# Moving a transpose from the matrix engine to VectorE and DMA in a two-layer graph kernel

## The chip, the cores and the metric

The kernel runs on one core of one Trainium2 chip. The metric is the device time of one execution in microseconds. Three executions of the kernel before took 2980.95 to 2983.51 us, with a median of 2982.35 us.

## What is computed

64 graphs of 256 nodes with 512 features, all in float32. Layer 0 is a graph network of three steps, layer 1 an attention whose weights are a softmax over the nodes; each layer ends with a residual sum and a layer norm.

```python
def _gcn_layer(x, adj, W, b):
    support = jnp.einsum('bnf,fh->bnh', x, W)
    return jnp.einsum('bnm,bmh->bnh', adj, support) + b

# layer 0
h = relu(_gcn_layer(x, adj, W1, b1)); h = relu(_gcn_layer(h, adj, W2, b2))
x1 = layernorm(x + _gcn_layer(h, adj, W3, b3))

# layer 1
q, k = split(x1 @ Wqk); v = x1 @ Wv
agg = einsum('bij,bjd->bid', adj, k * mask[:, :, None])
w = inv_scale * mask * einsum('bid,bid->bi', q, agg)
out = layernorm(x1 + softmax(w, axis=1)[:, :, None] * v)
```

The kernel uses q k^T = x1 M x1^T with M = Wq Wk^T, computed once. A score is then a row sum of (x1 M x1^T) times the adjacency.

## The kernel before

The graphs go through in 32 pairs (G = 2), one pair a pass, in a software pipeline over two pairs: pass i does layer 0 of pair i and, interleaved with it, the end of layer 0 and all of layer 1 of pair i-1. There is one pass more than there are pairs. Nodes are cut into NH = 2 halves of 128, features into DC = 4 chunks of 128.

A product of a pair with a 512x512 weight matrix is done by `seven` (L123 and L141 to L158): a Strassen-Winograd scheme with seven block products of four 128x128x256 products each, in place of eight. The left operand's sums S1, S2, S3, S4 are made by `left` (L108 to L111) on VectorE (DVE) and GpSimd (POOL); the weights' sums are constant. In `seven` the banks are X, Y, W, Z (bx, by, bw, bz). X is added to three times; after each time ScalarE (ACT) copies it out (u L141, v L147, t L152) before PE may add more, and DVE adds such a copy to Y, W, Z and writes the four quarters of the result. The quarter written last is the one of the bw drain (L158), which follows the last block product; the one before it comes from bz (L156).

The steps of a pass on TensorE (PE), in the order of the source:

- project W1 for pair i (L123), then pp (L199): the third adjacency product of pair i-1, 512 columns wide, drained and normalized by DVE in `layer0_out` and `layernorm` (L184 to L201) into x1, held in the tile xt
- pz (L175): the first adjacency product of pair i, drained with relu by ACT into hT
- px (L212): x1 of pair i-1 transposed on PE against an identity, 16 blocks of 128x128, copied out by ACT into x1T (L213)
- project W2 of pair i, then x1 M of pair i-1 (yT), then pz of the second step, then pg (L223), the scores' product yT x1T, whose drain on DVE (L228) makes w
- project W3 of pair i, then the softmax over the nodes: pw (L236, two small transposes), nmax on DVE (L238), e on ACT (L241, an exp), smx on DVE; then x1 Wv (vs), then ps (L251, the softmax back into columns), and on DVE `layer1_out`: the weighted sum, the layer norm and the store of xt to out (L262)

So each projection is followed on PE by a product that doesn't read its result, and each adjacency product by one that doesn't read its own.

Tiles come from pools with a fixed number of buffers: s, xt, an and mr have two, aT three, xT, x1T, yT, c and hT one. PSUM has seven banks with the tag "mm", taken in turn. The order of instructions on every engine is fixed when the kernel is built: a scheduler merges the steps and inserts waits on semaphores. All loads and stores are issued by SyncE (SP), in order. A DMA is counted on one of eight DMA semaphores in turn, so the ninth waits until the first has landed.

Of the kernel before, what the change touches and what calls it, by code (L numbers as in the profile page):

```python
# [9 lines left out]
FP = mybir.dt.float32  # L10
AF = mybir.ActivationFunctionType
OP = mybir.AluOpType
AX = mybir.AxisListType

P = 128
# [3 lines left out]
@with_exitstack  # L19
def gcn_then_graph_attention(ctx: ExitStack, tc: tile.TileContext, xT, xn, adjT, adjn, mask_row, mask_col,  # L20
                             W1, b1, W2, b2, W3, b3, WqT, WkT, Wv, out):

# [12 lines left out]
    nc = tc.nc  # L37
    NP, _, DC, G, N = xT.shape
    NH = N // P
    D = DC * P  # L40
    H = D // 2
# [6 lines left out]
    work = ctx.enter_context(tc.tile_pool(name="work", bufs=1))  # L48
# [39 lines left out]
    def load_w(w, name, eng):  # L88
        t = const.tile([P, 7, 2, H], FP, name=name)
        b12 = work.tile([P, 2, H], FP, name="b12", tag="t", bufs=2)  # L90
        nc.sync.dma_start(t[:, B11], w[:, 0:2, 0:H])
        nc.sync.dma_start(b12, w[:, 0:2, H:D])
        nc.sync.dma_start(t[:, B21], w[:, 2:4, 0:H])
        nc.sync.dma_start(t[:, B22], w[:, 2:4, H:D])
        combine_w(t, b12, eng)
        return t

# [1 line left out]

    def left(src, own, eng1, eng2, name, bufs=1):  # L100

        A11, A21 = src[:, 0:2, :, 0:P], src[:, 0:2, :, P:N]
        A12, A22 = src[:, 2:4, :, 0:P], src[:, 2:4, :, P:N]
        n = 4 if own else 3
        c = work.tile([P, n, 2, G, P], FP, name=name, bufs=bufs)
        S1, S2, S4 = c[:, 0], c[:, 1], c[:, 2]
        S3 = c[:, 3] if own else A21
        eng1.tensor_tensor(S1, A21, A22, op=OP.add)  # L108
        eng2.tensor_tensor(S3, A11, A21, op=OP.subtract)  # L109
        eng1.tensor_tensor(S2, S1, A11, op=OP.subtract)  # L110
        eng2.tensor_tensor(S4, A12, S2, op=OP.subtract)  # L111
        return dict(A11=A11, A12=A12, A22=A22, S1=S1, S2=S2, S3=S3, S4=S4)
# [14 lines left out]
    def seven(lf, w, dst, nodes_out):  # L127

        def bank(name):
            return psum.tile([P, 2, H], FP, name=name, tag="mm")  # L130

        def view(x):
            return x if nodes_out else x.rearrange("p o (g n) -> p o g n", g=G)

        def temp(name):
            return work.tile([P, 2, H], FP, name=name, tag=name, bufs=2)

        X = bank("bx")
        product(X, lf["A11"], w[:, B11], True, False, nodes_out)
        u = temp("u")  # L140
        nc.scalar.copy(u, X)  # L141
        Y = bank("by")
        product(Y, lf["A12"], w[:, B21], True, True, nodes_out)
        nc.vector.tensor_tensor(dst(0, 0), view(Y), view(u), op=OP.add)
        product(X, lf["S2"], w[:, T2], False, False, nodes_out)
        v = temp("v")
        nc.scalar.copy(v, X)  # L147
        W = bank("bw")
        product(W, lf["S3"], w[:, T3], True, False, nodes_out)
        product(X, lf["S1"], w[:, T1], False, True, nodes_out)  # L150
        t = temp("t")
        nc.scalar.copy(t, X)  # L152
        nc.vector.tensor_tensor(dst(1, 1), view(W), view(t), op=OP.add)  # L153
        Z = bank("bz")
        product(Z, lf["S4"], w[:, B22], True, True, nodes_out)
        nc.vector.tensor_tensor(dst(0, 1), view(Z), view(t), op=OP.add)  # L156
        product(W, lf["A22"], w[:, N4], False, True, nodes_out)
        nc.vector.tensor_tensor(dst(1, 0), view(W), view(v), op=OP.add)  # L158

    def project(lf, w, name, bufs):  # L160

        s = work.tile([P, G, NH, D], FP, name=name, bufs=bufs)
        seven(lf, w, lambda h, o: s[:, :, h, o * H:(o + 1) * H], True)
        return s


# [26 lines left out]

    def layer0_out(s, aT, xt):
        for g in range(G):
            for h in range(NH):
                pp = psum.tile([P, D], FP, name="pp", tag="mm")
                for m in range(NH):
                    nc.tensor.matmul(pp, lhsT=aT[:, g, m, h * P:(h + 1) * P], rhs=s[:, g, m, :],  # L199
                                     start=(m == 0), stop=(m == NH - 1))  # L200
                nc.vector.tensor_tensor(xt[:, g, h, :], pp, xt[:, g, h, :], op=OP.add)  # L201
            layernorm(xt, g)

    def transpose_x1(x1):
        x1T = work.tile([P, DC, G, N], FP, name="x1T")
        for g in range(G):
            for fp in range(DC // 2):
                pt = psum.tile([P, 2, N], FP, name="px", tag="mm")
                for j in range(2):
                    f = 2 * fp + j  # L210
                    for h in range(NH):
                        nc.tensor.transpose(pt[:, j, h * P:(h + 1) * P], x1[:, g, h, f * P:(f + 1) * P], ident)  # L212
                nc.scalar.copy(x1T[:, 2 * fp:2 * fp + 2, g, :], pt)  # L213
        return x1T

    def scores(i, yT, x1T, an):

        w = small.tile([P, NH, G], FP, name="w", bufs=2)
        for g in range(G):
            pg = psum.tile([P, NH, N], FP, name="pg", tag="mm")  # L220
            for h in range(NH):
                for d in range(DC):
                    nc.tensor.matmul(pg[:, h, :], lhsT=yT[:, d, g, h * P:(h + 1) * P], rhs=x1T[:, d, g, :],  # L223
                                     start=(d == 0), stop=(d == DC - 1))
            for h in range(NH):
                prod = work.tile([P, N], FP, name="prod")
                b = i * G + g
                nc.vector.scalar_tensor_tensor(prod, pg[:, h, :], mask_s[:, h, b:b + 1], an[:, g, h, :],  # L228
                                               op0=OP.mult, op1=OP.mult, accum_out=w[:, h, g:g + 1])
        return w  # L230
# [25 lines left out]
    def layer1_out(i, x1, v, s):  # L256
        for g in range(G):
            for h in range(NH):
                nc.vector.scalar_tensor_tensor(x1[:, g, h, :], v[:, g, h, :], s[:, h, g:g + 1], x1[:, g, h, :],
                                               op0=OP.mult, op1=OP.add)  # L260
            layernorm(x1, g)
        nc.sync.dma_start(out[i], x1)  # L262
# [34 lines left out]
    def make_m():  # L297
        b12 = work.tile([P, 2, H], FP, name="b12", tag="t", bufs=2)
        for f in range(DC):
            pt = psum.tile([P, 2, H], FP, name="pt", tag="mm")  # L300
            for d in range(DC):
                nc.tensor.matmul(pt, lhsT=qT[:, d, f * P:(f + 1) * P], rhs=kT[:, d, :],  # L302
                                 start=(d == 0), stop=(d == DC - 1))
            nc.scalar.copy(wm[:, B11 if f < 2 else B21, f % 2], pt[:, 0])
            nc.scalar.copy(b12[:, f % 2] if f < 2 else wm[:, B22, f % 2], pt[:, 1])
        combine_w(wm, b12, nc.gpsimd)

    V, PL = nc.vector, nc.gpsimd  # L310
    prev = None
    for i in range(NP + 1):
        new = i < NP
        if new:
            s = project(lx, w1, "s", 2)
        if prev is not None:
            xt, an = rest
            layer0_out(prev, aTs[i - 1], xt)
        if new:
            if i + 1 < NP:  # L320
                x0 = load_xT(i + 1)
                aTs[i + 1] = load_aT(i + 1)
            hT = aggregate_relu(s, aTs[i], bl1)
        if prev is not None:
            x1T = transpose_x1(xt)
        if new:
            s = project(left(hT, False, V, PL, "ch"), w2, "s", 2)
            if i + 1 < NP:
                lx = left(x0, False, PL, PL, "cx")
        if prev is not None:  # L330
            l1 = left(x1T, True, V, PL, "c1")
            yT = work.tile([P, DC, G, N], FP, name="yT")
            seven(l1, wm, lambda h, o: yT[:, 2 * o:2 * o + 2, :, h * P:(h + 1) * P], False)
        if new:
            hT = aggregate_relu(s, aTs[i], bl2)
        if prev is not None:
            w = scores(i - 1, yT, x1T, an)
        if new:
            s = project(left(hT, False, V, PL, "ch"), w3, "s", 2)
        if prev is not None:  # L340
            sm = softmax_rows(w)
            v = project(l1, wv, "vs", 1)
            layer1_out(i - 1, xt, v, softmax_cols(sm))
        if new:
            rest = load_rest(i)
        if i == 0:
            make_m()
        prev = s


# [40 lines left out]
```

## Time and profile before

The profiled execution took 2982.62 us, its span on the core 2980.8 us, at a mean granted TensorE clock of 0.996.

| group of the profile | count | busy us | mean ns |
|---|---|---|---|
| PE px, transposes (L212) | 512 | 74.9 | 283 |
| ACT x1T, their copies (L213) | 128 | 68.4 | 589 |
| PE pp, 512 columns (L199) | 512 | 225.1 | 592 |
| PE pz, 256 columns (L175) | 2048 | 453.6 | 379 |
| DVE L191, last step of the layer norm | 256 | 276.8 | 1123 |
| POOL L72, bias into xt | 32 | 145.4 | 4544 |
| DMA out, 1024 KB each | 32 | | 3900 to landing |

How to read it: each row is a group of instructions of one line; busy is their sum, the mean is one instruction's length as recorded. Matmuls are pipelined, so their recorded lengths overlap, and what a step takes is read from the starts of the steps in the timeline. A float32 product shows up as two instructions, a transpose as one. Over the span the 16 DMA engines are busy with 13.6% for the queue that SP issues on, and moved 149.24 MB there in 32864 packets.

### The profile page before, as it was taken

The page shows a single profiled execution, that of the slowest core. Times are in us where ns is not written, and L with a number is a line of the kernel's source. Part 1 is how long each engine was busy: PE and PEld are TensorE (multiplying, and loading weights), DVE is VectorE, ACT ScalarE, POOL GpSimd, SP SyncE. Part 2 cuts the span into 40 slices and gives each one's busy share as a digit, 9 for nine tenths or more (in the row PEclk, how much of TensorE's full clock was granted, in tenths as well). Part 3 has the DMA queues.
Part 4 walks back from the last instruction along what each step waited for, and adds up shares of the span by engine and source line. Part 5 has one row for each costly group of instructions (what it writes and reads, how often), then busy time and mean ns, then how long its engine had stood idle before and what let it go on. Part 6 is the DMA issues. An engine that isn't in the chain of part 4 may idle for free.

```text
span 2980.8 us, 32161 instructions
## 1 busy us (share of the span) xinstructions
PE 2926.8 (98%) x13216; PEld 2442.2 (82%) x13216; DVE 1363.5 (46%) x2386; ACT 661.5 (22%) x1130; POOL 698.1 (23%) x426
## 2 busy tenths in 40 slices
PE   8999999999999999999999999999999999999997
PEld 6788888888888888888888888888888888888885
DVE  3355334554345543455543455434555345554344
ACT  1222122222222222222212222222222122221221
POOL 4222022221222221222202222112222122221210
PEclk9999999999999999999999999999999999999998
DMA  5011101111011110111110111101111011111000
GB/s 195 22 61 61 46 25 57 53 61 60 11 60 50 60 61 26 45 57 54 60 54 18 60 50 60 61 11 60 50 61 60 32 39 57 53 60 50 8 29 28
DMA packets 33010, 151.29 MB, mean 51 GB/s; under 512 B 3680, under 2 KB 7904, under 8 KB 20320
## 3 DMA queue, kind: packets, MB, share of 16 engines
q1 hardware_dynamic: 32864, 149.24, 13.6%
q8 instruction: 104, 1.70, 0.2%
q14 instruction: 42, 0.34, 0.0%
HBM read 115.68 MB, written 33.55 MB: 50 GB/s over the span
## 4 chain that ended last, share of the span: by engine, by line
PE 90%; DVE 8%; DMA 1%; issue 1%; ACT 1%; POOL 0%; SPq 0%; DVEq 0%; POOLq 0%
PE bx L123 28%; PE bw L123 18%; PE pz L175 10%; PE bz L123 9%; PE by L123 9%; PE pg L223 7%; PE pp L199 6%; DVE xt L191 5%; DVE st L184 1%; PE px L212 1%; DVE xt L201 1%; DMA w<-in_W 1%; PE pt L302 0%; DMA xt<-in_xn 0%; DVE mv L185 0%
## 5 line engine op out<-in xcount | busy, mean ns | idle before, releaser
L175 PE MATMUL pz<-aT,s 128*128 128x256 f32 x2048 | 453.6, 379 | 0.0
L175 PEld LDWEIGHTS pz<-aT,s 128*128 128x128 f32 x2048 | 389.7, 190 | 66.7 <-issue 14.8
L109 POOL TENSOR_TENSOR hT<-hT 128x512 f32<-128x512 f32 x64 | 113.0, 1766 | 880.9 <-DVE ch L108 880.9
L108 POOL TENSOR_TENSOR cx<-xT 128x512 f32<-128x512 f32 x32 | 40.6, 1269 | 1024.9 <-DMA xT<-in_xT 990.0
L191 DVE TENSOR_SCALAR xt<-xt,mv,rs 128x512 f32<-128x512 f32 x256 | 276.8, 1123 | 1.2
L177 ACT ACTIVATE hT<-pz,bl 128x512 f32<-128x512 f32 x256 | 175.2, 685 | 400.8 <-PE pz L175 400.7
L123 PE MATMUL bw<-w,hT 128*128 128x256 f32 x1024 | 242.0, 379 | 1.6 <-POOL hT L109 1.6
L123 PE MATMUL bx<-w,ch 128*128 128x256 f32 x1024 | 242.0, 379 | 0.0
L153 DVE TENSOR_TENSOR s<-bw,t 128x512 f32<-128x512 f32 x96 | 66.4, 692 | 361.9 <-ACT t L152 361.9
L141 ACT COPY u<-bx 128x512 f32<-128x512 f32 x160 | 93.6, 585 | 612.7 <-PE bx L123 612.7
L223 PE MATMUL pg<-x1T,yT 128*128 128x256 f32 x1024 | 226.2, 379 | 0.0
L199 PE MATMUL pp<-s,aT 128*128 128x512 f32 x512 | 225.1, 592 | 0.0
L123 PEld LDWEIGHTS bw<-w,hT 128*128 128x128 f32 x1024 | 189.5, 190 | 33.4 <-POOL hT L109 2.0
L123 PEld LDWEIGHTS bx<-w,ch 128*128 128x128 f32 x1024 | 194.5, 190 | 26.6 <-issue 0.2
L223 PEld LDWEIGHTS pg<-x1T,yT 128*128 128x128 f32 x1024 | 194.6, 190 | 26.5
L152 ACT COPY t<-bx 128x512 f32<-128x512 f32 x160 | 93.6, 585 | 454.7 <-PE bx L123 447.4
L199 PEld LDWEIGHTS pp<-s,aT 128*128 128x128 f32 x512 | 97.2, 190 | 108.8 <-issue 107.1
L147 ACT COPY v<-bx 128x512 f32<-128x512 f32 x160 | 93.6, 585 | 406.5 <-PE bx L123 406.5
L184 DVE BATCH_NORM_STATS2 st<-xt 128x6 f32<-128x512 f32 x256 | 170.6, 688 | 2.1
L72 POOL TENSOR_TENSOR xt<-xt,bl 128x2048 f32<-128x2048 f32 x32 | 145.4, 4544 | 53.5 <-DMA xt<-in_xn 53.5
L108 DVE TENSOR_TENSOR ch<-hT 128x512 f32<-128x512 f32 x64 | 43.9, 686 | 234.5 <-ACT hT L177 234.5
L75 POOL TENSOR_TENSOR an<-an,mr 128x512 f32<-128x512 f32 x64 | 79.8, 1267 | 209.5 <-DMA an<-in_adjn 202.4
(108 smaller groups left out, 4543.2 us busy)
## 6 DMA issues: line engine op xcount, KB each, us to landing
xT<-in_xT SPq DMA_DIRECT2D x32, 1024.0 KB, 4.8
xt<-in_xn SPq DMA_DIRECT2D x32, 1024.0 KB, 6.9
out<-xt SPq DMA_DIRECT2D x32, 1024.0 KB, 3.9
aT<-in_adjT SPq DMA_DIRECT2D x32, 512.0 KB, 3.4
an<-in_adjn SPq DMA_DIRECT2D x32, 512.0 KB, 3.5
mr<-in_mask_row SPq DMA_DIRECT2D x32, 256.0 KB, 3.1
w<-in_W SPq DMA_DIRECT2D x9, 256.0 KB, 6.4
qT<-in_WqT SPq DMA_DIRECT2D x1, 1024.0 KB, 6.9
```

What stands on the lines that cost most here:

```text
L72: nc.gpsimd.tensor_tensor(xt.rearrange("p g h d -> p (g h) d"), xt.rearrange("p g h d -> p (g h) d"), bl3.unsqueeze(1).to_broadcast([P, G ...
L109: eng2.tensor_tensor(S3, A11, A21, op=OP.subtract)
L123: nc.tensor.matmul(bank[:, o], lhsT=lhsT, rhs=rhs, start=first and n == 0, stop=last and n == 3, skip_group_check=True)
L141: nc.scalar.copy(u, X)
L147: nc.scalar.copy(v, X)
L152: nc.scalar.copy(t, X)
L175: nc.tensor.matmul(pz[:, g, :], lhsT=s[:, g, m, f * P:(f + 1) * P], rhs=aT[:, g, m, :], start=(m == 0), stop=(m == NH - 1))
L177: nc.scalar.activation(hT[:, f], pz, AF.Relu, bias=bias[:, f:f + 1])
L184: nc.vector.bn_stats(st[:, h, :], x[:, g, h, :])
L191: nc.vector.tensor_scalar(x[:, g, h, :], x[:, g, h, :], mv[:, h, 0:1], rs[:, h:h + 1], op0=OP.subtract, op1=OP.mult)
L199: nc.tensor.matmul(pp, lhsT=aT[:, g, m, h * P:(h + 1) * P], rhs=s[:, g, m, :], start=(m == 0), stop=(m == NH - 1))
L223: nc.tensor.matmul(pg[:, h, :], lhsT=yT[:, d, g, h * P:(h + 1) * P], rhs=x1T[:, d, g, :], start=(d == 0), stop=(d == DC - 1))
```

## The change

x1 is no longer transposed on PE. In the new `transpose_x1` DVE transposes the 32x32 blocks of each 128x512 tile, each block where it stands (four instructions a pass, into the tile xs), and 16 DMAs from SP, each for one pair of partition groups, move the blocks to where a full transpose puts them (x1T). Each of these DMAs covers 32 partitions with 16 runs of 32 floats, from SBUF to SBUF. xs shares its buffer with yT. The layout of x1T changes from chunk, graph, node to graph, half, chunk, node, and `left` and `scores` index it so.

Softmax, x1 Wv and the rest of layer 1 become `attention_out` and are done one pass later, after the first pz of the next pass; the loop has one pass more. The source order of a pass is then W1, pp, pz, the late `attention_out`, W2, `transpose_x1`, pz, x1 M, W3, scores.

The column halves of every weight are loaded swapped and written swapped, so that `seven` completes columns 0 to 255 with its third drain and columns 256 to 511 with its fourth. pp runs in two halves of 256 columns, the first half of both node halves first.

```diff
-        nc.sync.dma_start(t[:, B11], w[:, 0:2, 0:H])
-        nc.sync.dma_start(b12, w[:, 0:2, H:D])
-        nc.sync.dma_start(t[:, B21], w[:, 2:4, 0:H])
-        nc.sync.dma_start(t[:, B22], w[:, 2:4, H:D])
+        nc.sync.dma_start(t[:, B11], w[:, 0:2, H:D])
+        nc.sync.dma_start(b12, w[:, 0:2, 0:H])
+        nc.sync.dma_start(t[:, B21], w[:, 2:4, H:D])
+        nc.sync.dma_start(t[:, B22], w[:, 2:4, 0:H])
...
-        seven(lf, w, lambda h, o: s[:, :, h, o * H:(o + 1) * H], True)
+        seven(lf, w, lambda h, o: s[:, :, h, (1 - o) * H:(2 - o) * H], True)
...
     def layer0_out(s, aT, xt):
         for g in range(G):
+            pps = [psum.tile([P, D], FP, name="pp", tag="mm") for h in range(NH)]
+            for o in range(2):
+                for h in range(NH):
+                    for m in range(NH):
+                        nc.tensor.matmul(pps[h][:, o * H:(o + 1) * H], lhsT=aT[:, g, m, h * P:(h + 1) * P],
+                                         rhs=s[:, g, m, o * H:(o + 1) * H], start=(m == 0), stop=(m == NH - 1))
             for h in range(NH):
-                pp = psum.tile([P, D], FP, name="pp", tag="mm")
-                for m in range(NH):
-                    nc.tensor.matmul(pp, lhsT=aT[:, g, m, h * P:(h + 1) * P], rhs=s[:, g, m, :],
-                                     start=(m == 0), stop=(m == NH - 1))
-                nc.vector.tensor_tensor(xt[:, g, h, :], pp, xt[:, g, h, :], op=OP.add)
+                nc.vector.tensor_tensor(xt[:, g, h, :], pps[h], xt[:, g, h, :], op=OP.add)
             layernorm(xt, g)
 
     def transpose_x1(x1):
-        x1T = work.tile([P, DC, G, N], FP, name="x1T")
+        Q = 32
+        xs = work.tile([P, G, NH, DC, P // Q, Q], FP, name="xs", tag="yT")
         for g in range(G):
-            for fp in range(DC // 2):
-                pt = psum.tile([P, 2, N], FP, name="px", tag="mm")
-                for j in range(2):
-                    f = 2 * fp + j
-                    for h in range(NH):
-                        nc.tensor.transpose(pt[:, j, h * P:(h + 1) * P], x1[:, g, h, f * P:(f + 1) * P], ident)
-                nc.scalar.copy(x1T[:, 2 * fp:2 * fp + 2, g, :], pt)
+            for h in range(NH):
+                nc.vector.transpose(xs[:, g, h].rearrange("p c b n -> p (c b n)"), x1[:, g, h, :])
+        x1T = work.tile([P, G, NH, DC, P], FP, name="x1T")
+        for nb in range(P // Q):
+            for fb in range(P // Q):
+                nc.sync.dma_start(
+                    x1T[fb * Q:(fb + 1) * Q, :, :, :, nb * Q:(nb + 1) * Q].rearrange("p g h c n -> p (g h c) n"),
+                    xs[nb * Q:(nb + 1) * Q, :, :, :, fb, :].rearrange("p g h c n -> p (g h c) n"))
         return x1T
...
-    prev = None
-    for i in range(NP + 1):
+    def attention_out(i, l1, xt, w):
+        sm = softmax_rows(w)
+        v = project(l1, wv, "vs", 1)
+        layer1_out(i, xt, v, softmax_cols(sm))
+
+    prev, late = None, None
+    for i in range(NP + 2):
...
-        if prev is not None:
-            x1T = transpose_x1(xt)
+        if late is not None:
+            attention_out(*late)
+            late = None
         if new:
             s = project(left(hT, False, V, PL, "ch"), w2, "s", 2)
             if i + 1 < NP:
                 lx = left(x0, False, PL, PL, "cx")
         if prev is not None:
+            x1T = transpose_x1(xt)
+        if new:
+            hT = aggregate_relu(s, aTs[i], bl2)
+        if prev is not None:
             l1 = left(x1T, True, V, PL, "c1")
             yT = work.tile([P, DC, G, N], FP, name="yT")
-            seven(l1, wm, lambda h, o: yT[:, 2 * o:2 * o + 2, :, h * P:(h + 1) * P], False)
-        if new:
-            hT = aggregate_relu(s, aTs[i], bl2)
+            seven(l1, wm, lambda h, o: yT[:, 2 - 2 * o:4 - 2 * o, :, h * P:(h + 1) * P], False)
+        if new:
+            s = project(left(hT, False, V, PL, "ch"), w3, "s", 2)
         if prev is not None:
             w = scores(i - 1, yT, x1T, an)
-        if new:
-            s = project(left(hT, False, V, PL, "ch"), w3, "s", 2)
-        if prev is not None:
-            sm = softmax_rows(w)
-            v = project(l1, wv, "vs", 1)
-            layer1_out(i - 1, xt, v, softmax_cols(sm))
+            late = (i - 1, l1, xt, w)
```

In the order as built, a steady pass has on SP six of the 16 block moves, then the store to out, then the other ten, then the loads of xt, an and mr; on DVE the four block transposes stand before nmax, and nmax before the copies for W2's left sums; on POOL the bias addition into xt stands after the sums c of x1T.

## The prediction

> **What bounds the kernel now.** I read the busy shares first, then PE's waits, then one pass in the timeline.
>
> ```profile
> span 2980.8 us, 32161 instructions
> ...
> PE 2926.8 (98%) x13216; PEld 2442.2 (82%) x13216; DVE 1363.5 (46%) x2386; ACT 661.5 (22%) x1130; POOL 698.1 (23%) x426
> ```
>
> PE is busy 98% of the span and no other engine half of it. The view of waits, cut to PE, holds only this:
>
> ```profile
> PE px L212 <- DVE xt L191: 19.3, 30, 1.5
> PE bx L123 <- DMA w<-in_W: 7.3, 1, 7.3
> PE px L212 <- issue: 5.8, 1, 5.8
> PE bw L123 <- DVE s L153: 3.7, 1, 3.7
> PE bw L123 <- POOL hT L109: 1.6, 1, 1.6
> ```
>
> So a change pays only if it takes work from PE or makes PE wait. The only repeated wait, 30 times, stands before the transposes px. The timeline of one pass, PE alone, from project W1 (start 995.80) on:
>
> ```profile
> 1008.00 7.03 PE L199 MATMUL pp<-s,aT 128*128 128x512 f32 x16
> 1014.86 7.07 PE L175 MATMUL pz<-aT,s 128*128 128x256 f32 x32
> 1021.77 1.04 PE L212 MATMUL px<-ident,xt 128*128 128x128 f32 x8
> 1023.25 1.44 PE L212 MATMUL px<-ident,xt 128*128 128x128 f32 x8 [0.45 <-DVE xt L191]
> 1024.53 1.89 PE L123 MATMUL bx<-w,hT 128*128 128x256 f32 x8
> ```
>
> The transposes hold PE from 1021.77 to 1024.53, 2.76 us with their wait. The next pass begins at 1087.22: 91.42 us a pass, 32 such passes. Other lengths from starts in the same view: a projection of 28 products 12.1 us, pz or pg 6.9, pp 6.86.
>
> **What the Trainium skill says.** "VectorE: DVE Perf Modes", The three transpose paths: VectorE transposes 32x32 blocks only, 311 ns for a 128x128 bf16 tile; no transpose on VectorE is in this trace. "DMA: Bandwidth & Descriptors", Specifications: below 512 B a transfer is read, modified and written; its section Why small descriptors are slow says that SBUF to SBUF does not suffer, 128-byte packets still reaching 78% of the link. The two pull apart, and nothing here is 128 B. The same page, Queues, rings and completion order: each DMA engine consumes its descriptors in ring order. "TensorE: Matmul & The Clock Gate", Part 1: after an idle window of some 3.4 us the array runs at half clock for about as long. The trace agrees: PE idles from 21 to 24.7 us, and the stretches 26 to 29 us show a granted clock of 0.50.
>
> **The change part by part.** Times below are inside one steady pass, 0 where W1 starts.
>
> *Transposes off PE.* 16 px a pass go: -2.76. pp becomes 32 products of 256 columns instead of 16 of 512; pz has that form and takes 6.91 against 6.86: +0.05. Net -2.71, times the 31 passes that have a following W2: -84. ACT loses four copies of 0.59, which nobody waited for.
>
> *New order on PE.* W1 0, pp 12.2, pz 19.1, pw 26.0, x1Wv of the pass before 26.3 to 38.4, ps, W2 38.6 to 50.7, pz 50.7 to 57.6, x1M 57.6, W3, pg. Formerly x1M lay between W2 and the pz that reads its result; now pz follows W2 directly. The swapped halves deal with that: columns 0 to 255 are complete with the bz drain, which in the trace is done 0.9 us after bz, and the last product bw takes 1.73; pz's first two groups then take 3.46 while bw drains. Cost 0. The same few drains sit behind layer 1's chain on DVE, as they did behind W1 before (bz drained at 1006.47, bw ended 1008.16), so this cover holds.
>
> *Softmax before x1Wv.* The exp e stands on ACT ahead of u, the copy of x1Wv's first bank, and PE may add into that bank again only after u. Two products cover it: u must be done by 26.3+3.46 = 29.8. e waits for nmax, and DVE has nmax behind all four transposes. DVE: first add 14.9 (its bank is now full after 6 of 8 product groups), group 0 normalized by 21.3, as long as before since POOL's cx still collides with it (2.62 us for the L191 pair at 1014.68); group 1 adds and statistics to 24.1; two transposes; the L191 pair now about 1.0 since POOL's xt addition L72 (4.52 us, which stretched it to 4.25) has moved behind c; two transposes. A transpose of 128x512: the skill's 311 ns less 133 for 128 columns at one a cycle leaves 178, plus 533 gives 0.71 (estimate); bn_stats of the same size takes 0.69. So nmax starts about 28.3, e 28.7 (ACT: hT, then a table load of 1.28, also till 28.7), its 0.65, u 0.58: 30.0. I charge 0.4 a pass. Bounds: 0, and 2.6 if a transpose takes two cycles a column (1.3).
>
> *Block moves.* 16 DMAs a pass, each 32 partitions x 16 rows of 128 B, all from SP's queue. x1T has one buffer, last read by x1Wv, so they start at its end, E = 38.4. In the built order six go, then out, then ten. The out waits for layer 1:
>
> ```profile
> 1085.19 1.89 PE L123 MATMUL bw<-wv,x1T 128*128 128x256 f32 x8
> 1087.72 0.15 DVE L253 COPY s<-ps 128x4 f32<-128x4 f32 x1
> 1094.85 0.99 DVE L191 TENSOR_SCALAR xt<-xt,mv,rs 128x512 f32<-128x512 f32 x2
> 1095.87 0.34 SPq L262 DMA_DIRECT2D out<-xt  x1
> ```
>
> That is (bw done at 1087.1) 8.8 us after x1Wv, and the ten blocks stand behind it on SP. Cutting the DMA view to 1095 to 1099.5 shows out's data until 3.2 us after its issue; the engines take the blocks after that: E+12.0. The ten are 320 rows per engine. Each engine's price d of a 128 B row: in the saturated stretch 5 to 20 us,
>
> ```profile
> DMA packets 3690, 5.49 MB, mean 366 GB/s; under 512 B 517, under 2 KB 3305, under 8 KB 3433
> ...
> q1 hardware_dynamic: 3690, 5.49, 102.9%
> ```
>
> 1.029x16x15 = 247 engine-us; at the 437 GB/s that the adjn load peaks at, 27.3 per engine, the bytes take 201; the other 46 over 3690 packets are 12.5 ns each, and 128 B adds 4.7: 17 ns. Read-modify-write might double it: 34. Below: 5, bytes alone. Above: the lone loads of 2 KB (15.5% of 16 engines over 7 us, 144 packets: 121 ns) and 4 KB (26.5% over 6 us, 144: 177 ns) give by a straight line 65 at nothing, so about 68. I take 22, above the saturated figure because of the skill's remark. The last block lands at E+12.0+0.32d+0.6 = E+19.6. x1M wants x1T at 57.6 = E+19.2. Stall 0.4. Issue is no limit: ten of about 0.45 (128 rows 0.34, 256 rows 0.38 at start) from E+9.2. DVE (c, L108) and POOL (c, L109) wait at the heads of their queues for the same landing; behind them are only yT drains and the next xt addition. S2 needs 1.25+1.65 after landing, PE gives it 3.46. SP sits on the first block from about 19 to E; the next loads (xt, an) come behind the blocks and are due a pass later.
>
> *The end.* After the last layer 0 nothing is left to run under the moves. Before: pp end (2924.65) to 2980.8 is 56.2, plus the x1Wv that stood ahead of pp, 12.3: 68.5. After: x1Wv 12.1 and about 2.8 for a copy late behind two table loads, 19.6 for the blocks, x1M 12.1 and 1.5 for the halved clock, pg 6.9, x1Wv 12.5, DVE and out 13.1: 80.6. So +12.
>
> **Sum.** The profiled execution took 2982.6, 0.3 above the median of the runs. 2982.6-84+12 = 2910.6; 30 passes have both stalls, 30x(0.4+0.4) = 24: 2935. Break-even is at 2.4 us of stall a pass.
>
> **Rivals.**
>
> *A. Blocks late behind out.* For: the margin is nothing, one SP wait holds ten of the sixteen, and the row size is not in the trace. The stall is 0.32d-6.6 a pass; it decides from d = 27, where it is 2.0 and together with the 0.4 reaches break-even. At d = 34 it is 4.3, and about 1.7 more once the array has cooled: 2910.6+30x6.4 = 3103. At 68 it is 15.2+1.7: some 3430. Against: the saturated stretch says 17. Chance 0.30.
>
> *B. Softmax late.* Transposes at two cycles: 2910.6+30x(2.6+0.4) = 3001. For: e ahead of u on ACT. Against: bn_stats at a column a cycle. Chance 0.06.
>
> *C. Both about 1 us too long*, 2910.6+30x2.4 = 2982: no change. Chance 0.05.
>
> *D. Nothing waits*: d near 5 to 17 and u on time: 2910 to 2920, the low end of the forecast.
>
> **How the numbers follow.** The forecast with D has 0.59, its own range is 2900 to 2965 (stalls from 0 to 1.5 a pass, the end 5 to 20). A has 0.30, B 0.06, C 0.05. About 0.2%, 6 us, is what can be told from no change. Faster 0.59, same 0.05, slower 0.36. Below 2900 I leave 0.05; the range goes up to 3110, d about 34, and leaves some 0.14 above.
>
> **What would show it.** px gone from PE and the 2.76 with it; four DVE transposes near 0.7 each; bx of Wv waiting for u by under 1 us; bx of x1M waiting for the block DMAs by under 1.5 us, out issued between them 8.8 us after x1Wv; pz after W2 with no wait; 12 us more at the end. Wrong if PE waits for the DMA x1T by several microseconds in each pass, with a granted clock under 1 after it, or if 8192 packets of 128 B a pass hold the engines for more than about 27 ns each.

## The result, and the profile after

The changed kernel takes 3007.99 us (median of 4 runs, 3005.99 to 3009.08); the kernel before, run on the same chip, 2981.67 (2980.95 to 2983.51). The ratio is 1.0087, its 95% interval 1.0069 to 1.0104: slower by 26 us. The forecast was 2935, faster by 47.

The top of the page of the kernel after:

```profile
span 3007.3 us, 32865 instructions
...
PE 2892.8 (96%) x13216; PEld 2499.3 (83%) x13216; DVE 1354.0 (45%) x2514; ACT 589.6 (20%) x1002; POOL 699.2 (23%) x426
```

PE is busy 34 us less than before (2926.8), in a span that is 26 us longer. So it waits. The mean granted clock fell too, from 0.996 to 0.985. The view of waits, cut to PE (total, times, longest):

```profile
PE bx L130 <- DVE c L117: 64.8, 31, 2.3
PE bx L130 <- DMA x1T<-xs: 19.1, 1, 19.1
...
PE bx L130 <- issue: 2.6, 5, 0.6
PE bx L130 <- ACT hT L184: 1.6, 2, 0.8
```

The waits before the transposes (19.3 us, 30 times) are gone. In their place is a wait in each of 31 passes for c, the second sum S2 of x1T on DVE: 2.28 us in 24 of them. In the other seven x1M itself starts 0.35 to 0.84 late (the last two rows, 4.2 us together). The view gives these to other causes, but each of the seven starts comes 0.4 to 0.5 us after the last block has landed, and there the wait for c is shorter by about as much (1.2 to 1.7), so that the pass is no longer for it. Only at the end is a wait for the blocks long. The timeline of PE around that wait, in one pass:

```profile
1026.47 1.89 PE L130 MATMUL bw<-wv,x1T 128*128 128x256 f32 x8
...
1040.69 7.07 PE L182 MATMUL pz<-aT,s 128*128 128x256 f32 x32
1047.60 1.89 PE L130 MATMUL bx<-x1T,wm 128*128 128x256 f32 x8
1049.33 1.89 PE L130 MATMUL by<-x1T,wm 128*128 128x256 f32 x8
1053.50 1.97 PE L130 MATMUL bx<-c,wm 128*128 128x256 f32 x8 [2.28 <-DVE c L117]
```

pz and the first two products of x1M follow one another without a gap: x1T has landed by 1047.60 (at 1047.06, by the record of the last move). The third product, the first to read a sum of x1T, starts 4.17 us after the second instead of 1.73. DVE in the same stretch:

```profile
1048.59 0.69 DVE L115 TENSOR_TENSOR ch<-hT 128x512 f32<-128x512 f32 x1 [7.00 <-ACT hT L184]
1049.32 0.69 DVE L117 TENSOR_TENSOR ch<-ch,hT 128x512 f32<-128x512 f32 x1
1049.93 1.75 DVE L115 TENSOR_TENSOR c<-x1T 128x512 f32<-128x512 f32 x1
1051.72 1.63 DVE L117 TENSOR_TENSOR c<-c,x1T 128x512 f32<-128x512 f32 x1
```

Here is the cause. DVE idles 7.00 us, and not for x1T: ahead of c in its queue stands ch, the sums of hT for W3, and hT is the result of the pz that ends on PE at 1047.8. In the source the sums of x1T stand before those for W3; in the order as built they stand behind them, on DVE and on POOL. The Trainium skill, "TensorE: Matmul & The Clock Gate", its table of specifications, calls the queue of VectorE a strict FIFO; the trace agrees: c does not overtake ch, though its input is there from 1047.06 and ch starts only at 1048.59. The chain of waits walks the same way back, from c to the end of pz (start, length, what):

```profile
1040.86 6.92 PE pz L182 x32
...
1047.80 0.70 ACT hT L184
...
1048.59 0.70 DVE ch L115
...
1049.93 1.77 DVE c L115
```

The kernel before had the same order on DVE. From its trace:

```profile
1023.58 0.68 DVE L108 TENSOR_TENSOR ch<-hT 128x512 f32<-128x512 f32 x1
1024.29 0.69 DVE L110 TENSOR_TENSOR ch<-ch,hT 128x512 f32<-128x512 f32 x1
1025.40 1.25 DVE L108 TENSOR_TENSOR c<-x1T 128x512 f32<-128x512 f32 x1 [0.42 <-ACT x1T L213]
1026.69 1.65 DVE L110 TENSOR_TENSOR c<-c,x1T 128x512 f32<-128x512 f32 x1
```

There it cost nothing: ch was for W2, which ran on PE ahead of x1M (c was made twelve microseconds before it was read). The change moved the pz that makes hT to a place directly ahead of x1M, and with it made c wait for hT.

POOL, which makes S3 and S4, has a share in the length of the wait. Its sums of hT run beside c:

```profile
1049.36 1.77 POOL L116 TENSOR_TENSOR hT<-hT 128x512 f32<-128x512 f32 x1 [27.86 <-DVE ch L115]
1051.10 1.71 POOL L118 TENSOR_TENSOR ch<-hT,ch 128x512 f32<-128x512 f32 x1
```

Each of the two sums of c starts on DVE while one of these is running and ends 0.55 us after it, so they take 1.75 and 1.63 where ch takes 0.69. With 0.69 for each, c would be done about 2.0 us earlier (estimate: 3.38 - 1.38), which is most of the 2.28. No run keeps POOL off DVE with the order left as it is, so this share isn't shown.

The wait has a second price. In 14 of the 29 passes between the second and the 31st pp, and in the last one, PE runs slower after it. The timeline of PE in such a pass:

```profile
590.82 2.52 PE L130 MATMUL bx<-c,wm 128*128 128x256 f32 x8 [2.28 <-DVE c L117]
593.13 3.06 PE L130 MATMUL bw<-c,wm 128*128 128x256 f32 x8
```

and the busy time there by stretches (us, PE busy, granted clock, share of the DMA engines, GB/s):

```profile
592.09:595.50 3.41, 3.41 (x10) 0.50 0.00 0
684.25:687.66 3.41, 3.41 (x10) 0.50 0.00 0
597.00:602.00 5.00, 5.00 (x25) 1.00 0.00 0
```

bw takes 3.06 in place of 1.89. From one pp to the next these passes take about 92.89, the others 91.21, so the lowered clock costs 1.68 each time.

Which passes are hit isn't left to chance. Each lowered stretch lasts 3.41 us, and all 15 starts lie whole multiples of 3.413 us apart: from 592.09 to 684.25, the two stretches above, it is 92.16, or 27 times 3.413. Laid on this grid, the 31 waits for c here and the 31 of the run e1 below fall in two groups. Where 2.08 us or more of a wait lie in one interval of the grid, the next interval runs at half clock (32 of 32); where it is 1.94 or less, it doesn't (30 of 30). A wait of 2.28 us, placed at random, has 2 us in one interval about half the time (estimate: (3.41 - 2.28 + 2 x 0.27) / 3.41 = 0.49).

The sum, from the starts of pp: the first comes 1.05 us later (94.38 against 93.33), the last 2922.09 - 94.38 = 2827.71 after the first instead of 2824.28 (+3.43), and the rest is 85.21 instead of 63.19 (+22.02). Of the rest 12.5 is the one x1 Wv that moved out of the passes. So the passes cost 3.43 + 12.5 = 15.9 and the end 9.5; with the start, 26.5, the difference of the two spans.

### The profile page after: what moved, and what is told of

The parts are those of the page before. It is cut to its first block, busy times and chain, and to the rows that moved or that the text cites. A ratio compares the mean times of both kernels' runs of the same rounds, so it can differ in the third digit from the quotient of the medians.

```text
span 3007.3 us, 32865 instructions
## 1 busy us (share of the span) xinstructions
PE 2892.8 (96%) x13216; PEld 2499.3 (83%) x13216; DVE 1354.0 (45%) x2514; ACT 589.6 (20%) x1002; POOL 699.2 (23%) x426
## 4 chain that ended last, share of the span: by engine, by line
PE 92%; DVE 5%; issue 1%; DMA 1%; ACT 1%; POOL 0%; SPq 0%; DVEq 0%; POOLq 0%
PE bx L130 27%; PE bw L130 18%; PE pz L182 14%; PE bz L130 9%; PE pg L235 7%; PE pp L207 7%; PE by L130 7%; DVE c L115 2%; DVE c L117 2%; DVE ch L115 1%; ACT hT L184 1%; DMA w<-in_W 1%; PE pt L314 0%; DMA xt<-in_xn 0%; SPq L223 0%
## 5 line engine op out<-in xcount | busy, mean ns | idle before, releaser
L207 PE MATMUL pp<-s,aT 128*128 128x256 f32 x1024 | 226.2, 379 | 0.0
L207 PEld LDWEIGHTS pp<-s,aT 128*128 128x128 f32 x1024 | 194.6, 190 | 26.5
L235 PEld LDWEIGHTS pg<-x1T,yT 128*128 128x128 f32 x1024 | 194.6, 190 | 26.5
L130 PE MATMUL bx<-c,wm 128*128 128x256 f32 x512 | 143.9, 431 | 64.8 <-DVE c L117 64.8
L130 PEld LDWEIGHTS bx<-c,wm 128*128 128x128 f32 x512 | 106.7, 214 | 92.5 <-issue 76.4
L198 DVE TENSOR_SCALAR xt<-xt,mv,rs 128x512 f32<-128x512 f32 x256 | 176.8, 732 | 2.4
```

The lines of the kernel that those rows point to most:

```text
L130: nc.tensor.matmul(bank[:, o], lhsT=lhsT, rhs=rhs, start=first and n == 0, stop=last and n == 3, skip_group_check=True)
L198: nc.vector.tensor_scalar(x[:, g, h, :], x[:, g, h, :], mv[:, h, 0:1], rs[:, h:h + 1], op0=OP.subtract, op1=OP.mult)
L207: nc.tensor.matmul(pps[h][:, o * H:(o + 1) * H], lhsT=aT[:, g, m, h * P:(h + 1) * P], rhs=s[:, g, m, o * H:(o + 1) * H], start=(m == 0), s ...
```

## The experiments

Theories: (1) the queue's order: c waits behind ch; (2) the landing: the last ten block moves, behind the store to out, reach x1T too late and c follows; (3) the softmax or the halves of pp hold a pass; this one had no run of its own, since PE shows no gap at either place. "c first" below means that ch is put behind c on DVE and POOL; line numbers move by two or three there. The runs are on three chips; the kernel before took 2982.28 to 2983.25 us beside them, so medians of different runs can be compared to about 1 us.

### The store on another queue (e1)

```diff
-        nc.sync.dma_start(out[i], x1)
+        nc.scalar.dma_start(out[i], x1)
```

> The store to out goes to ACT's queue, so all 16 block moves follow each other on SP; the order on DVE and POOL stays, with the sums ch of hT ahead of the sums c of x1T. Theory 1 (c stands behind ch on DVE): the blocks land about 5 us earlier, but PE still waits 2.28 us a pass for c L117 and the clock stays near 0.985; only the end gains some 5 us: about 3002 us (2995 to 3008). Theory 2 (the blocks land too late): the wait goes, 31 x 2.28 and the slow clock's 24 us with it: about 2912 us.

3012.27 us, ratio to before 1.0101 (1.0086 to 1.0116), above the 2995 to 3008 that was expected. SP now issues all 16 moves in a row. The last block lands at 1045.24 instead of 1047.06, 1.8 us sooner where 5 had been expected:

```profile
1028.39 15.41 SPq L223 DMA_DIRECT2D x1T<-xs  x16
1043.91 0.56 SPq L71 DMA_DIRECT2D xt<-in_xn  x1
```

The waits of PE in this kernel:

```profile
PE bx L130 <- DVE c L117: 70.6, 31, 2.3
PE bx L130 <- DMA x1T<-xs: 17.0, 1, 17.0
```

The wait in the passes is what it was, now 2.28 in all 31, and c on DVE starts at 1049.92 as in the kernel after (1049.93). x1M never starts late here. The wait at the end is 2.1 us shorter, but 17 of the 31 waits have the lowered clock behind them instead of 15 (2 x 1.68 = 3.4 us). Theory 2 falls.

### c first (e2)

The sums of hT for W3 are issued behind those of x1T; nothing else changes.

```diff
-            s = project(left(hT, False, V, PL, "ch"), w3, "s", 2)
+            with ExitStack() as after_c:
+                if prev is not None:
+                    for ins in c_ins:
+                        after_c.enter_context(tc.issue_after(ins.ins))
+                lh = left(hT, False, V, PL, "ch")
+            s = project(lh, w3, "s", 2)
```

> The sums c of x1T are put ahead of the sums ch for W3 on DVE and on POOL, nothing else moves; the store stays between the block moves. Theory 1: PE's wait for c falls from 2.28 us to under 0.3 a pass, the granted clock returns to 0.995 or more, a pass takes 88.9 us: 3008 - 71 - 24 = 2913 us (2903 to 2930). Theory 2: c now waits for the last block, a wait of about 2 us stays and the time is near 3000.

2911.41 us, ratio 0.9763 (0.9747 to 0.9779), clock 0.994. DVE:

```profile
1016.51 0.69 DVE L117 TENSOR_TENSOR c<-x1T 128x512 f32<-128x512 f32 x1 [5.58 <-DMA x1T<-xs]
1017.23 1.65 DVE L119 TENSOR_TENSOR c<-c,x1T 128x512 f32<-128x512 f32 x1
1018.81 0.68 DVE L117 TENSOR_TENSOR ch<-hT 128x512 f32<-128x512 f32 x1
```

Now c waits for the landing and for nothing else, and is done before the third product starts (1020.39). The first sum takes 0.69 instead of 1.75: no sum of POOL is running when it starts (POOL's first starts at 1016.54). Most passes take 88.69 instead of 91.21 or 92.89. One order of two pairs of sums, on DVE and POOL together, is worth 97 us: theory 1 holds. The landing has little to spare: c starts on it at 1016.51, and x1M at 1016.94. Six of 29 passes take 0.6 to 0.9 more. In all six x1M starts 0.3 to 0.7 late, 0.3 to 0.5 us after the last block has landed, and in the first of them SP is held longer by its ten moves (9.00 instead of 8.07):

```profile
473.19 9.00 SPq L226 DMA_DIRECT2D x1T<-xs  x10
```

### The gap filled (e3)

This separates the wait from the lowered clock. Five products that nobody needs are put on PE where it waits, in the kernel after.

```diff
+        if fill:
+            dummy = psum_s.tile([P, H], FP, name="dummy", tag="sm")
+            for k in range(fill):
+                nc.tensor.matmul(dummy, lhsT=lf["A22"][:, 0, 0, :], rhs=w[:, B11, 0, :], start=True, stop=True)
         product(X, lf["S2"], w[:, T2], False, False, nodes_out)
```

> Five unneeded products (2.16 us of PE) run on PE between x1M's second and third block product, inside the wait of 2.28 us; their result is read by nobody. Theory 1, with the half clock as an answer to the idle stretch: the wait for c stays but is filled, the granted clock returns to 0.995, about 24 us go: 2984 us (2978 to 2990). Rival (the clock falls for another reason, such as load or the DMA traffic): clock 0.985 and 3008 us, or more.

2989.73 us, ratio 1.0024 (1.0014 to 1.0035): 18 us less than the kernel after, with more work. PE in one pass:

```profile
1041.81 1.89 PE L130 MATMUL by<-x1T,wm 128*128 128x256 f32 x8
1043.53 2.32 PE L155 MATMUL dummy<-wm,x1T 128*128 128x256 f32 x10
1045.99 1.97 PE L130 MATMUL bx<-c,wm 128*128 128x256 f32 x8
1047.79 1.89 PE L130 MATMUL bw<-c,wm 128*128 128x256 f32 x8
```

The place is held as long as before, and 24 of 29 passes take 91.2; the longest takes 92.04 (x1M starts 0.95 late there), and the mean clock is 0.994. The time is within the 2978 to 2990 that was expected. So the extra 1.68 us is a consequence of PE's idle time; c is as late as before.

### c first, and the store on ACT's queue (e4)

Both edits above.

> Both edits: c ahead of ch, and the store on ACT's queue. Theory 1: as with c ahead alone, less about 5 us at the end: 2908 us (2898 to 2922). Theory 2: also near 2910, so this one tells only whether the late blocks cost anything once c is first: more than 8 us below c ahead alone would say so.

2905.41 us, ratio 0.9744 (0.9729 to 0.9758). What gained nothing alone is worth 6 us once c is first, less than the 8 that the expectation had asked for as a sign. Of the 6.7 us between the two spans, 3.3 lie in the passes, 2.6 at the end and 0.8 at the start. DVE and PE (two views):

```profile
1012.40 0.69 DVE L117 TENSOR_TENSOR c<-x1T 128x512 f32<-128x512 f32 x1 [3.87 <-DMA x1T<-xs]
```

```profile
1014.55 1.89 PE L133 MATMUL bx<-x1T,wm 128*128 128x256 f32 x8
```

c starts on the landing 2.1 us before x1M, and 25 of 29 passes take 88.69, the other four 0.28 more.

### The old halves (e5)

c first, with the column halves of the weights and of the results as they were before (pp keeps its two halves).

```diff
-        seven(lf, w, lambda h, o: s[:, :, h, (1 - o) * H:(2 - o) * H], True)
+        seven(lf, w, lambda h, o: s[:, :, h, o * H:(o + 1) * H], True)
```

> On the kernel with c first (2911 us), the swap of the column halves is undone: columns 0 to 255 are again completed by the last drain; pp keeps its halves. Theory (the order of the halves hides the last drain): each pz after W2 waits for that drain, 0.2 + 0.7 us after the last product, 31 x 0.9 = 28 us, so about 2939 us (2930 to 2948), the clock staying at 0.994 since the idle stretch is short. Rival (the drain was hidden anyway): 2911 us.

2915.18 us, ratio 0.9775 (0.9759 to 0.9791), where 2939 had been expected: a miss. Most passes take 88.88, 0.19 more than e2. The expectation had pz wait for a whole half of columns. The drain that comes last now writes the quarter of these columns that belongs to the second node half, and pz's first two products read the first: the drain ends at 1010.65, and the fifth instruction of pz, due at 1010.62, starts at 1010.71. So swapping the halves brings 0.19 us a pass (4 us of medians).

### No delay (e6)

c first, with softmax, x1 Wv and the rest of layer 1 back in their own pass after W3, and pg directly after x1M.

```diff
-        if late is not None:
-            attention_out(*late)
-            late = None
...
+        if prev is not None:
+            attention_out(i - 1, l1, xt, w)
```

> On the kernel with c first, x1Wv and the softmax go back into their own pass, after W3, and pg goes to the place after x1M; the block moves no longer wait for x1Wv. Theory (the delay is needed as cover between pz and W2): the four block transposes and the slow L191 pair stand ahead of ch on DVE, W2's third product waits about 2 us a pass for ch and the clock falls in about half the passes: 2911 + 60 + 22 = 2993 us (2960 to 3010). Rival (the delay buys nothing): 2911 us or some 5 less.

2951.65 us, ratio 0.9896 (0.9881 to 0.9911): slower than e2 as expected, but by 40 instead of 80, below the range of 2960 to 3010. PE:

```profile
1012.73 1.96 PE L133 MATMUL bx<-w,ch 128*128 128x256 f32 x8 [1.20 <-DVE ch L119]
1014.53 1.89 PE L133 MATMUL bw<-w,hT 128*128 128x256 f32 x8
```

Without x1 Wv between pz and W2, the sums for W2 stand behind the layer norm and the four transposes on DVE, and PE waits for them: 33.1 us in 29 waits. In place of the 2 us a pass that had been expected, a wait is 0.9 to 1.2 us (1.8 once), and the lowered clock didn't come in the passes: no such wait has 2 us in one interval of the grid, and the product after the one shown takes its full-clock 1.89. The delay does pay, since it gives DVE 12 us in which to finish x1. The edit also moves pg and frees the block moves from x1 Wv; what each does alone isn't separated.

### The transposes back on PE (e7)

c first, transposes on PE between W2 and pz with copies on ACT, no block moves.

```diff
-                nc.vector.transpose(xs[:, g, h].rearrange("p c b n -> p (c b n)"), x1[:, g, h, :])
+                pt = psum.tile([P, DC, P], FP, name="px", tag="mm")
+                for f in range(DC):
+                    nc.tensor.transpose(pt[:, f, :], x1[:, g, h, f * P:(f + 1) * P], ident)
+                nc.scalar.copy(x1T[:, g, h], pt)
```

> On the kernel with c first, the transposes go back to PE, between W2 and pz, with their copies on ACT; order, delay and halves stay. This prices the transposes alone. Theory: 16 px take 1.73 us of PE a pass where nothing waits (the first pass of the kernel before shows 1.73), 31 x 1.73 = 54, and the end is some 13 us shorter since no block moves lie open there: 2911 + 54 - 13 = 2952 us (2942 to 2960). Rival (a transpose on PE costs the 2.76 us of the usual pass before): 2911 + 86 - 13 = 2984 us.

2947.10 us, ratio 0.9881 (0.9867 to 0.9896). PE:

```profile
1026.64 1.91 PE L223 MATMUL px<-ident,xt 128*128 128x128 f32 x16
1028.39 7.07 PE L185 MATMUL pz<-aT,s 128*128 128x256 f32 x32
```

The 16 transposes hold PE for 1.75 us, and every pass takes 90.44 against 88.69. This kernel has neither DVE transposes nor moves and still gains 35 us on the kernel before. So of the 2.76 that px held PE in the pass shown before, 1.75 was transposing. The other 1.0, of which the profile records 0.45 as a wait for xt, goes once the transposes stand behind the late x1 Wv and W2.

### The last pass on PE (e8)

e4, with the last x1T, which has no W2 and pz above it, transposed on PE.

```diff
-            x1T = transpose_x1(xt)
+            x1T = transpose_x1(xt) if new else transpose_x1_pe(xt)
```

> c first and the store on ACT as before, and in the last pass alone, where no new pair follows, x1 is transposed on PE with copies on ACT, as the kernel before did. Theory: the end's 17.1 us wait for the blocks, with nothing left to cover it, is the whole price of the moves that is left, and it lies open. It is replaced by some 2 us of transposes and about 2 us for the first left sums, which wait for DVE behind the rest of the layer's end: 2905 - 13 = 2892 (2885 to 2900). Rival: the end is bound elsewhere (the layer norm and store of the pair before stand ahead on DVE and are needed first): no change, 2905.

2893.82 us (2892.62 to 2894.55), ratio 0.9700 (0.9684 to 0.9717): the fastest of all. The end in the kernel after, on PE:

```profile
2941.40 0.28 PE L263 MATMUL ps<-ident,smx 2*128 2x2 f32 x2
2960.81 3.71 PE L130 MATMUL bx<-x1T,wm 128*128 128x256 f32 x8 [19.13 <-DMA x1T<-xs]
```

and in this one:

```profile
2840.04 0.28 PE L276 MATMUL ps<-ident,smx 2*128 2x2 f32 x2
2840.25 1.97 PE L222 MATMUL px<-ident,xt 128*128 128x128 f32 x16
2842.60 1.99 PE L133 MATMUL bx<-x1T,wm 128*128 128x256 f32 x8 [0.39 <-ACT x1T L223]
2844.43 1.89 PE L133 MATMUL by<-x1T,wm 128*128 128x256 f32 x8
2846.16 1.89 PE L133 MATMUL bw<-c,wm 128*128 128x256 f32 x8
2850.02 1.97 PE L133 MATMUL bx<-c,wm 128*128 128x256 f32 x8 [1.98 <-DVE c L119]
```

From ps to x1M it is 2.6 us instead of 19.4, and the halved first product (3.71) is gone. Some is given back: c comes late behind layer 1's end on DVE (1.98 of wait), and the last product of x1M waits 1.46 for yT. The net gain over e4 is 11.6 us of medians, near the 13 expected. The rival, an end bound by something else, falls: the wait for the blocks at the end had nothing to cover it.

## Why the prediction was wrong

**The step that failed** is in the part on the block moves: "DVE (c, L108) and POOL (c, L109) wait at the heads of their queues for the same landing; behind them are only yT drains". c wasn't at the head. ch stood ahead of it and waited for the hT of the pz that the change had put directly before x1M. The next sentence, "S2 needs 1.25+1.65 after landing, PE gives it 3.46", had a length near the measured one (2.90 against 1.75 + 1.63 = 3.38, both within the 3.46) and the wrong start: 1049.93 instead of the landing at 1047.06. The text asked what stood behind c and didn't ask what stood ahead of it in the order as built. The rows to see it were there: pz's end plus about 0.9 for its last drain (as the text had for bz's), two sums of ch (1.4), two of c (2.9), less 3.46, is 1.7 us a pass. The measured wait is 2.28; counted from start to start, the pass is 2.52 longer (91.21 - 88.69).

**The lowered clock** was priced in rival A, for waits of 4.3 us, and not for one of about two. Its size there, "about 1.7", was right; it came after 15 of 31 waits, 15 x 1.68 = 25 us. With 31 x 2.52 = 78 us the one wait cost 103; e2, which removes it, gains 97 of the span. Of the difference, 4.4 are its own six late passes and 1.7 its start and end. The break-even of "2.4 us of stall a pass" stands: 103/31 = 3.3 lies above it.

**px off PE**: right. A pass without waits takes 88.69 (e2, e4), 2.8 less than the 91.5 of before; the sum had 2.71. What the sum didn't separate, e7 did: only 1.75 of it needed the transposes moved.

**Swap of the halves at 0 cost**: right, pz follows W2 without a gap; but its worth is 0.19 us a pass, not the cover of a whole drain.

**Softmax**: right in that it isn't a cause, and its 0.4 didn't come: the products of x1 Wv start at 1016.11, 1017.84 and 1019.56 with no gap in the pass shown. Each DVE transpose takes 0.68 in the mean (0.71 was the estimate), so rival B is out.

**Landing**: the time was nearly right, by luck. x1T was to land 19.6 us after the end E of x1 Wv (1028.2 in the pass shown); it lands at E + 18.9, and x1M wants it at E + 19.4. In place of a stall of 0.4 in every pass there are the seven late starts, which the wait for c hides. But "Issue is no limit" was wrong. From the trace after, SP:

```profile
1028.39 4.23 SPq L223 DMA_DIRECT2D x1T<-xs  x6
1037.15 0.35 SPq L274 DMA_DIRECT2D out<-xt  x1
1037.54 8.09 SPq L223 DMA_DIRECT2D x1T<-xs  x10
```

Ten moves hold SP 8.09 us, 0.81 each where 0.45 was taken, and the last is out at 1045.63, E + 17.4. From 1041 to 1046 the 16 engines are busy 71.7% with 4198 packets: 0.717 x 16 x 5 / 4198 = 13.7 ns a packet, nearly all of them rows of 128 B, below the 22 taken and below the 27 from which rival A decides. Two errors of opposite sign made nearly the right sum. The store was issued 8.95 us after E (8.8 predicted).

**The end**: +12 predicted, +9.5 measured, and the wait of 19.1 there was 19.6 in the sum.

**The rivals**: the result is near rival B's 3001 by accident and in no part by its mechanism. The true rival (a sum of another step ahead in the same queue) wasn't among them.

## What to carry to other kernels

When a step is moved on one engine, go through every other engine's queue and ask of each instruction that feeds the moved step or its new neighbour what stands ahead of it and what that waits for; an order that was harmless while its producer ran early becomes a wait when the producer moves next to the consumer. A gap of two microseconds in PE may cost nearly twice its length (2.28 and 1.68 here), and whether it does depends on where it falls, so a small wait deserves its own line in the sum. And an experiment that removes a second suspect alone, as e1, can show nothing until the first is gone (e4).

## What was not expected of the hardware

- A wait of 2.28 us on PE was followed by a halved clock in 15 of 31 cases, and after the waits of 1.2 us in e6 the clock stays at 1.00. The Trainium skill, "TensorE: Matmul & The Clock Gate", Part 1, speaks of an idle window of about 3.4 us that runs freely. The trace agrees on the length and on the free running (a grid of 3.413 us, whatever the kernel does), but the window need not be idle throughout: 2.08 us of it were enough, and 1.94 were not.
- 128-byte rows from SBUF to SBUF took 13.7 ns each in the mean on engines that were not full, below the 12.5 + 4.7 read from the saturated loads; no doubling shows. That agrees with the Trainium skill, "DMA: Bandwidth & Descriptors", Why small descriptors are slow, against the reading of its specifications that a row under 512 B might double.
- Issuing one move of 512 such rows holds SP 0.70 (six), 0.81 (ten) or 0.96 us (16 in a row, e1). Whether this is its own work or the queue pushing back wasn't tried.
- A DVE sum of 128x512 takes 0.69 when no POOL instruction is running as it starts, even if one starts beside it. When one is running, the sum ends 0.55 us after POOL's instruction does, in all 65 such sums of c and ch in the kernel after (0.545 to 0.553); a sum of c then takes 1.63 to 1.77. So the one that starts first seems to hold the other up, and the order of the two queues sets the length of the sums.
